# A two-layer block with routed experts: the first expert weight gather moved ahead of the row scatters, and the scattered rows normalised one chunk at a time

## The chip, the cores and the metric

The kernel runs on one core of a Trainium2 chip. The metric is the device time of one execution in microseconds (us). Three runs of the kernel before took 2112.46, 2118.58 and 2127.67 us, so the median is 2118.58 us.

The engines go by the short names of the profile: PE is the matrix engine, DVE the vector engine, ACT the scalar engine, POOL the general-purpose engine that here also issues all indirect (gathering and scattering) DMAs, and SP the engine that issues the plain ones.

## What is computed

The input is x, 8 sequences of 512 tokens with 256 features, in float32. There are two layers. Each normalises its input and adds an attention and a feed-forward part of the normalised rows to it. Layer 0, which the change touches, is cut to this:

```python
xn = layernorm(x)
x = x + attention(xn) + experts(xn)

# experts(xn), a row at a time
aff = xn @ centroids.T              # 8 experts
e = argmax(aff); alpha = sigmoid(aff[e])
h = layernorm(xn, ln_g[e], ln_b[e]) # a row that is normed a second time
y = xn + relu(h @ w1[e].T + b1[e]) @ w2[e].T + b2[e]
out = alpha * y + (1 - alpha) * xn
```

The second layer is two rounds of causal attention with a convolution between them, and a low-rank feed-forward part.

## The kernel before, in words

Tokens are held as 8 batches (`acc[b]`) of 4 chunks of 128 rows, 32 chunks in all. Layer 0 runs a fixed order of steps (`run`). Attention has 32 jobs (a batch and a group of four heads each) of 8 steps; job j's exponentials begin at step 12 + 8j, and its last product ends at step 20 + 8j. In each step the program issues score matmuls (L345 for the maxima, L394 for the exponentials), then `fill` puts other work into the step, then the products with the values (L434) follow. The work that `fill` takes comes from a list with due times (projections, transposed maxima) and from a generator, `stream`. The generator holds, in order: norms and affinities of the 8 batches (`FIRST`, 8 steps), `routing`, the experts, and the start of the second layer (`SECOND`). Where the generator yields `At(t)` nothing more is taken from it before step t; where it yields a number, that is a cost against an allowance of 2.08 a step. All engines work through their own instructions in the order of the program; waits between them are put in by the framework, one for each thing that an instruction needs.

**The rows that are scattered.** `first_norm` (L589) makes the once-normed rows of a batch on ACT (L257), and the twice-normed rows `h0` of four chunks on POOL (L596), into one of eight buffers that stay until the scatter. This happens in the first 53 us.

**Routing.** `routing` (L665) works out on DVE where each row goes (`pos_i`, L728) and which rows of the weight table each expert block needs (`wrow_i`, L738). Then, one chunk a step and 32 times, POOL issues an indirect DMA that scatters the 128 rows of the chunk to `hs_d` in DRAM (L741), and then a scaling of the chunk in place (`first_sum`, L608). Every scatter writes `hs_d`, and so the framework makes each wait for the one before it to land. At the same place in POOL's order stand the sums of finished attention jobs (L899).

**The experts.** When the 32 scatters have been issued, the pool `pre`, which holds `h0` among other things, is closed, and the pool `moe` takes its memory; a tile of `moe` waits for the tiles of `pre` that lay in its place. `Block(moe, 0)` (L753) issues on POOL the gather of the first block's weights (L756, 128 rows of 17,456 bytes) and on SP the load of its 256 rows of `hs_d` (L763). After `At(todo.t + 5)`, five steps later, `features` transposes these rows on PE (L772) and scales them on DVE with columns of the gathered weights (L777). `hidden` (L794, L805, L807) and `output` (L815, L824) follow. There are 23 blocks of 256 rows. The weights of block n + 1 are gathered while block n is worked on, in two buffers of `moe`. The sums of the blocks go to DRAM (L826), and `SECOND` gathers them back (L512), ends layer 0 and begins layer 1.

Of the kernel before, what the change touches and what calls it, by code (L numbers as in the profile page):

```python
# [9 lines left out]
F32 = mybir.dt.float32  # L10
# [3 lines left out]
ALU = mybir.AluOpType  # L14
# [5 lines left out]
P = 128  # L20
NB = 8
S = 512
D = 256
NC = S // P
# [26 lines left out]
ROW = O_B2 + D  # L51
# [101 lines left out]
def block_kernel(ctx: ExitStack, tc: tile.TileContext, x, a0_wqk, a0_bqk, a0_wv, a0_bv, cent, experts,  # L153
                 a1_wqk, a1_bqk, a1_wv, a1_bv, conv_w, conv_b, out_w, out_b, u1, v1, f_b1, u2, v2, f_b2, out):
    nc = tc.nc
# [11 lines left out]
    acc = []  # L167
# [13 lines left out]
    for i in range(2):  # L181
        half = mask_t[:, i * P : (i + 1) * P]
        nc.gpsimd.affine_select(
            out=half, in_=half, pattern=[[1, P]], compare_op=ALU.is_ge, fill=NEG, base=0, channel_multiplier=-1
# [18 lines left out]
    def bank(kind="mm"):  # L203
        rings[kind].append(rings[kind].pop(0))
        return rings[kind][-1]
# [12 lines left out]
    def banks_experts():  # L218
        share_banks(mx=banks[:2], sc=banks[4:6], av=banks[6:7], mm=banks[2:4] + banks[7:])
# [320 lines left out]
    wrow_i = const.tile([P, NBLK], I32, name="wrow_i")  # L540
# [24 lines left out]
    with ExitStack() as l0:  # L565
# [12 lines left out]
        nc.scalar.dma_start(out=cent_sb[:, :, :NE], in_=cent)  # L578

        later = ExitStack()  # L580
        pre = later.enter_context(tc.tile_pool(name="pre", bufs=1))
        aff = pre.tile([P, NT, NE], F32, name="aff")
        zeros = pre.tile([P, 2 * D], F32, name="zeros")
        nc.gpsimd.memset(zeros, 0.0)
        hs_z = hs_d.rearrange("(n p r) d -> n p (r d)", p=P, r=2)
        h0 = []
        firsts0 = {}

        def first_norm(norms, i):  # L589
            b = norms.bs[i]  # L590
            xn = work.tile([P, NC, D], F32, tag="o", name=f"xn{b}")
            norms.norm(i, xn)
            h = pre.tile([P, NC, D], F32, tag="h0", name=f"h0_{b}", bufs=NB)
            for c in range(NC):
                n = i * NC + c
                nc.gpsimd.tensor_scalar(  # L596
                    h[:, c, :], acc[b][:, c, :], norms.rs[:, 1, n : n + 1], norms.nm2[:, n : n + 1],
                    ALU.mult, ALU.add,
                )
                firsts0[b, c] = norms, n  # L600
            h0.append(h)
            return xn

        def first_sum(b, c):

            norms, n = firsts0[b, c]
            a = acc[b][:, c, :]
            nc.gpsimd.tensor_scalar(a, a, norms.rs1[:, n : n + 1], norms.nm_t[:, n : n + 1], ALU.mult, ALU.add)  # L608
# [27 lines left out]
        def pt(shape, name, tag=None, bufs=1):  # L636
            return pre.tile(shape, F32, name=name, tag=tag or name, bufs=bufs)
# [27 lines left out]
        def routing():  # L665

            mx = pt([P, NT], "mx")
            nc.vector.tensor_reduce(mx, aff, AX.X, ALU.max)
            nc.scalar.activation(alpha, mx, AF.Exp, scale=-1.0)
            nc.vector.tensor_scalar(alpha, alpha, 1.0, None, ALU.add)  # L670
            nc.vector.reciprocal(alpha, alpha)
            eq = pt(sh, "eq", "place")
            nc.vector.tensor_tensor(eq, aff, mx.unsqueeze(2).to_broadcast(sh), ALU.is_equal)
            cand = pt(sh, "cand", "rank")
            nc.vector.scalar_tensor_tensor(
                cand.rearrange(flat), eq.rearrange(flat), -float(NE), iota_e.rearrange(flat), ALU.mult, ALU.add
            )
            idx = pt([P, NT], "idx")
            nc.vector.tensor_reduce(idx, cand, AX.X, ALU.min)
            nc.vector.tensor_scalar(idx, idx, float(NE), None, ALU.add)  # L680
            oh = pt(sh, "oh")
            nc.vector.tensor_tensor(oh, iota_e, idx.unsqueeze(2).to_broadcast(sh), ALU.is_equal)
            yield At(todo.t + 1)


            ps = bank()
            psr, pst = ps[:, : NT * NE], ps[:, NT * NE :]
            nc.tensor.matmul(psr, lhsT=upper, rhs=oh.rearrange(flat), start=True, stop=True)
            nc.tensor.matmul(pst, lhsT=all_one, rhs=oh.rearrange(flat), start=True, stop=True)
            tot = pt(sh, "tot_sb")  # L690
            nc.vector.tensor_copy(tot.rearrange(flat), pst)
            cum = tot
            step = 1
            while step < NT:
                nxt = pt(sh, f"cum{step}", "cum", 2)
                nc.vector.tensor_tensor(nxt[:, step:, :], cum[:, step:, :], cum[:, : NT - step, :], ALU.add)
                nc.vector.tensor_copy(nxt[:, :step, :], cum[:, :step, :])
                cum = nxt
                step *= 2
            rank = pt(sh, "rank_sb", "rank")  # L700
            nc.vector.tensor_tensor(rank.rearrange(flat), cum.rearrange(flat), psr, ALU.add)
            yield At(todo.t + 2)

            gt = pt([P, NE, NB * S // TB], "gt")
            nc.vector.tensor_tensor(
                gt, cum[:, NT - 1, :].unsqueeze(2).to_broadcast([P, NE, NB * S // TB]), thr, ALU.is_gt
            )
            nblk = pt([P, NE], "nblk")
            nc.vector.tensor_reduce(nblk, gt, AX.X, ALU.add)
            ends = nblk  # L710
            step = 1
            while step < NE:
                nxt = pt([P, NE], f"ends{step}")
                nc.vector.tensor_tensor(nxt[:, step:], ends[:, step:], ends[:, : NE - step], ALU.add)
                nc.vector.tensor_copy(nxt[:, :step], ends[:, :step])
                ends = nxt
                step *= 2
            start = pt([P, NE], "start")
            nc.vector.tensor_tensor(start, ends, nblk, ALU.subtract)
            nc.vector.tensor_scalar(start, start, float(TB), None, ALU.mult)  # L720

            place = pt(sh, "place")
            nc.vector.tensor_tensor(place, rank, tot, ALU.subtract)
            nc.vector.tensor_tensor(place, place, start.unsqueeze(1).to_broadcast(sh), ALU.add)
            nc.vector.tensor_tensor(place, place, oh, ALU.mult)
            pos = pt([P, NT], "pos")
            nc.vector.tensor_reduce(pos, place, AX.X, ALU.add)
            nc.vector.tensor_copy(pos_i, pos)  # L728
            yield At(todo.t + 1)


            ge = pt([P, NBLK, NE], "ge")
            nc.vector.tensor_tensor(ge, iota_b, ends.unsqueeze(1).to_broadcast([P, NBLK, NE]), ALU.is_ge)
            wrow = pt([P, NBLK], "wrow")
            nc.vector.tensor_reduce(wrow, ge, AX.X, ALU.add)
            nc.vector.tensor_scalar(wrow, wrow, float(NE - 1), float(P), ALU.min, ALU.mult)
            nc.vector.tensor_scalar(wrow, wrow, iota_p, None, ALU.add)
            nc.vector.tensor_copy(wrow_i, wrow)  # L738

            for t in range(NT):  # L740
                nc.gpsimd.indirect_dma_start(  # L741
                    out=hs_d[:, :],
                    out_offset=IndirectOffsetOnAxis(ap=pos_i[:, t : t + 1], axis=0),
                    in_=h0[t // NC][:, t % NC, :],
                    in_offset=None,
                )
                first_sum(t // NC, t % NC)
                yield At(todo.t + 1)

        class Block:  # L750


            def __init__(self, moe, n):  # L753
                self.moe, self.n = moe, n
                self.w = moe.tile([P, ROW], F32, tag="w", name=f"w{n}")
                nc.gpsimd.indirect_dma_start(  # L756
                    out=self.w[:, :],
                    out_offset=None,
                    in_=experts,
                    in_offset=IndirectOffsetOnAxis(ap=wrow_i[:, n : n + 1], axis=0),  # L760
                )
                self.hs = moe.tile([P, TB // P, D], F32, tag="hs", name=f"hs{n}", bufs=1)
                nc.sync.dma_start(  # L763
                    out=self.hs, in_=hs_d[n * TB : (n + 1) * TB, :].rearrange("(j p) d -> p j d", p=P)
                )
# [64 lines left out]
        def stream():  # L830
# [7 lines left out]
            def norm(b):  # L838
                xns[b] = first_norm(*of[b])
# [17 lines left out]
            moe = later.enter_context(tc.tile_pool(name="moe", bufs=2, reuse_waits="tile"))  # L857
# [3 lines left out]
            nc.sync.dma_start(out=fb2_sb, in_=f_b2)  # L861
            nc.gpsimd.tensor_tensor(ob_sb, ob_sb, fb2_sb, ALU.add)
            nxt = Block(moe, 0)
            yield At(todo.t + 5)
            banks_experts()
            nxt.features()
            yield 0.5
# [18 lines left out]
        todo = Work()  # L886
# [48 lines left out]
        norms = [Norms(pre, bs, nm, True) for bs, nm in (((0,), "a"), ((1, 2, 3), "b"), ((4, 5, 6, 7), "e"))]  # L935
# [25 lines left out]
    with tc.tile_pool(name="ffn", bufs=1, side="right", reuse_waits="tile") as ffn:  # L961
# [53 lines left out]
        for n, (b, c2) in enumerate(pairs):  # L1015
# [6 lines left out]
            _, _, hT = ahead.pop(0)  # L1022
# [11 lines left out]
    for i in range(2):  # L1034
        t = l1.tile([P, 2, S + 2], F32, tag=f"ctxT{i}", name=f"ctxT{i}", bufs=1)
# [7 lines left out]
        out=cmask[:, S - P :], in_=cmask[:, S - P :], pattern=[[-1, P]], compare_op=ALU.is_ge, fill=NEG, base=0,  # L1043
# [224 lines left out]
```

## Time and profile before

The profiled execution took 2120.86 us. Its span, from its first instruction to its last, is 2118.7 us. The mean granted PE clock is 0.974 of full speed.

| engine | busy us | share of the span | instructions |
|---|---|---|---|
| PE, matmuls | 2010.6 | 95% | 13672 |
| DVE | 1228.6 | 58% | 3565 |
| ACT | 867.8 | 41% | 1690 |
| POOL | 175.6 | 8% | 222 |

| operation on or from POOL | count | mean us of one |
|---|---|---|
| L596, twice-normed rows of a chunk | 32 | 0.56 |
| L741, issue of a scatter | 32 | 1.04, landing 2.5 after its start (median) |
| L608, scaling of a chunk | 32 | 0.55 to 0.57 |
| L756, issue of a weight gather | 23 | 0.96, landing 9.5 after its start (median) |
| L899, sum of an attention job | 32 | 0.73 |

How to read it: an instruction is named by its line in the kernel, its engine and `out<-in`. An idle time is put down to what ended it. The chain of waits goes back from the last instruction: at each step to what released it. "issue" in it is time in which an engine waited for nothing that the profile shows. A DMA's issue is an instruction; its landing is later. DMA engines are shared by all queues.

### The profile page before, as it was taken

The numbers are of one execution on the slowest core, as the hardware profiler recorded it, in microseconds if no ns is written. First come the engines' busy times: TensorE is split into PE (matmuls) and PEld (weight loads), VectorE is DVE, ScalarE is ACT, GpSimd is POOL, SyncE is SP. The second block draws the span as 40 slices with busy tenths as digits, with TensorE's granted clock in tenths as the row PEclk, the third lists the DMA queues.
The fourth block names the chain that finished last, engine by engine and source line by source line (L and its number), as shares of the span: only waits on it lengthen the run. The fifth ranks groups of instructions, "written<-read, shape, count | busy, mean of one in ns | idle before, by whom it ended". The sixth has DMA issues, their size and how long they took to land.

```text
span 2118.7 us, 35530 instructions
## 1 busy us (share of the span) xinstructions
PE 2010.6 (95%) x13672; PEld 1016.4 (48%) x13672; DVE 1228.6 (58%) x3565; ACT 867.8 (41%) x1690; POOL 175.6 (8%) x222
## 2 busy tenths in 40 slices
PE   5797999999999999998898999999999999999998
PEld 3333555555555555552233445455555545554554
DVE  5564455555555555557424676666766666666763
ACT  4342333333333333335551444444444444444434
POOL 4153000000000000004211000000000000000000
PEclk8698999999999999999999899999999999999999
DMA  6014212212121221202100000000000000000000
GB/s 211 13 45 143 104 54 105 101 58 105 53 105 53 105 105 53 105 11 78 40 1 1 2 2 2 2 2 12 2 12 2 12 2 12 2 11 2 2 12 21
DMA packets 37192, 93.53 MB, mean 44 GB/s; under 512 B 5920, under 2 KB 28064, under 8 KB 34080
## 3 DMA queue, kind: packets, MB, share of 16 engines
q0 software_dynamic: 6384, 59.78, 7.7%
q1 hardware_dynamic: 29792, 30.56, 4.5%
q8 instruction: 107, 1.75, 0.3%
q10 hardware_dynamic: 848, 0.93, 0.1%
q14 instruction: 61, 0.50, 0.1%
HBM read 70.03 MB, written 20.45 MB: 43 GB/s over the span
## 4 chain that ended last, share of the span: by engine, by line
PE 83%; DVE 6%; issue 5%; DMA 4%; ACT 2%; POOL 1%; ACTq 0%; POOLq 0%; DVEq 0%; SPq 0%
PE bank L345 27%; PE bank L434 12%; PE bank L794 8%; PE bank L815 8%; PE bank L293 5%; PE bank L1072 4%; PE bank L412 4%; DMA hs_d<-h,pos_i 4%; PE bank L394 3%; PE bank L303 2%; PE bank L1090 2%; PE bank L1124 1%; DVE m L362 1%; PE bank L977 1%; PE bank L990 1%
## 5 line engine op out<-in xcount | busy, mean ns | idle before, releaser
L421 ACT ACTIVATE e<-bank 128x512 f32<-128x512 f32 (+1 forms) x1280 | 638.9, 552 | 921.4 <-PE bank L394 462.8
L345 PE MATMUL bank<-k,q 32*128 32x512 f32 (+3 forms) x3072 | 765.1, 538 | 24.6 <-DVE m L362 20.3
L394 PE MATMUL bank<-q,k 32*128 32x512 f32 (+3 forms) x3072 | 682.6, 535 | 2.4 <-DVE m L362 1.6
L365 DVE CUSTOM_DVE_ANT_0 jk<-bank,cmask 128x512 bf16<-128x512 f32 (+3 forms) x1024 | 502.8, 491 | 241.7 <-PE bank L345 162.4
L345 PEld LDWEIGHTS bank<-k,q 32*128 32x128 f32 x3072 | 301.4, 187 | 388.4 <-issue 165.2
L362 DVE TENSOR_REDUCE m<-bank 128x1 f32<-128x512 f32 x512 | 328.8, 685 | 152.5 <-PE bank L394 122.7
L434 PE MATMUL bank<-e,v 128*32 128x512 f32 (+3 forms) x3072 | 317.8, 501 | 0.7 <-ACT e L421 0.7
L394 PEld LDWEIGHTS bank<-q,k 32*128 32x128 f32 x3072 | 266.0, 186 | 12.2 <-issue 6.1
L794 PE MATMUL bank<-hsT,w 128*128 128x256 f32 x736 | 181.2, 392 | 6.4 <-DVE hsT L777 6.4
L794 PEld LDWEIGHTS bank<-hsT,w 128*128 128x128 f32 x736 | 135.1, 192 | 74.5 <-issue 58.9
L815 PE MATMUL bank<-w,hT 128*128 128x256 f32 x736 | 170.7, 385 | 0.0
L815 PEld LDWEIGHTS bank<-w,hT 128*128 128x128 f32 x736 | 137.5, 192 | 36.6 <-issue 18.7
L434 PEld LDWEIGHTS bank<-e,v 128*32 128x32 f32 x3072 | 67.7, 108 | 139.7 <-issue 133.0
L412 PE MATMUL bank<-mask_t,ident_bf 128*128 128x128 bf16 (+1 forms) x768 | 123.4, 244 | 0.0
L412 PEld LDWEIGHTS <-ident_bf 128*128 128x128 bf16 x768 | 43.9, 97 | 155.7 <-issue 140.6
L807 DVE TENSOR_SCALAR hT<-bank,w 128x256 f32<-128x256 f32 x92 | 44.5, 484 | 113.7 <-ACT hT L805 113.7
L1072 PE MATMUL bank<-ctxT,cw_sb 128*128 128x256 f32 x384 | 90.0, 383 | 2.1 <-DVE q L283 1.8
L365 DVE DVE_READ_ACCUMULATOR2_ANT m<- 128x1 f32 x1024 | 85.0, 83 | 0.0
L805 ACT ACTIVATE hT<-bank,w 128x256 f32<-128x256 f32 x92 | 43.7, 475 | 92.9 <-PE bank L794 92.9
L824 DVE TENSOR_TENSOR f<-bank,w 128x256 f32<-128x256 f32 x46 | 19.5, 425 | 105.4 <-PE bank L815 105.4
L285 ACT ACTIVATE k<-bank,bqk,rows 128x512 f32<-128x512 f32 x64 | 46.3, 774 | 81.7 <-PE bank L293 72.4
L1072 PEld LDWEIGHTS bank<-ctxT,cw_sb 128*128 128x128 f32 x384 | 70.1, 189 | 13.2 <-DVE q L283 3.2
(186 smaller groups left out, 1383.5 us busy)
## 6 DMA issues: line engine op xcount, KB each, us to landing
q<-mT SPq DMA_DIRECT2D x384, 2.0 KB
hs_d<-zeros SPq DMA_DIRECT2D x23, 256.0 KB
hs<-hs_d SPq DMA_DIRECT2D x23, 256.0 KB
fs_d<-f SPq DMA_DIRECT2D x23, 256.0 KB
acc<-in_x SPq DMA_DIRECT2D x8, 512.0 KB
out<-acc SPq DMA_DIRECT2D x8, 512.0 KB
cw_sb<-in_conv_w SPq DMA_DIRECT2D x1, 768.0 KB
wqk<-in_a_wqk ACTq DMA_DIRECT2D x1, 512.0 KB
```

What stands on the lines that cost most here:

```text
L285: nc.scalar.activation(dst, ps, AF.Identity, bias=bias[:, half : half + 1], scale=rows[:, half : half + 1])
L293: nc.tensor.matmul(ps, lhsT=w[:, k, col : col + P], rhs=src[:, k, :], start=(k == 0), stop=(k == 1))
L345: lambda h=h, qc=qc, at=at, nk=nk: nc.tensor.matmul(heads[h % 2][:, at : at + nk], lhsT=self.q[h * PH : (h + 1) * PH, qc * P : (qc + 1) * ...
L362: nc.vector.tensor_reduce(self.m[:, qc, h, :], src, AX.X, ALU.max, negate=True)
L365: nc.vector.tensor_tensor_reduce(out=junk[:, :nk], in0=src, in1=cmask[:, S - nk :], scale=1.0, scalar=-3e38, op0=ALU.add, op1=ALU.max, acc ...
L394: lambda h=h, kc=kc, at=at, lo=lo: nc.tensor.matmul(heads[h % 2][:, at : at + S - lo], lhsT=self.k[h * PH : (h + 1) * PH, kc * P : (kc + 1 ...
L412: nc.tensor.matmul(heads[h][:, : len(blocks) * P], lhsT=ident_bf, rhs=mask_t[:, : len(blocks) * P], start=False, stop=True,)
L421: nc.scalar.activation(e[:, h, :], heads[h][:, :n], AF.Exp, scale=self.scale)
L434: nc.tensor.matmul(self.av[h * PH : (h + 1) * PH, lo:], lhsT=self.v[:, kc, 4 * self.g + h, :], rhs=es[h // 2][:, h % 2, :], start=first, s ...
L794: nc.tensor.matmul(ps[:, i * TB : (i + 1) * TB], lhsT=w[:, O_W1 + k * FF + fc * P : O_W1 + k * FF + (fc + 1) * P], rhs=self.hsT[:, k, :], ...
L815: nc.tensor.matmul(ps[:, 0:D], lhsT=self.hT[:, fc, j * P : (j + 1) * P], rhs=w[:, O_W2 + fc * D : O_W2 + (fc + 1) * D], start=(fc == 0), s ...
L1072: nc.tensor.matmul(ps[:, :w], lhsT=cw_sb[:, k, tap, c * P : (c + 1) * P], rhs=ctxT[b % 2][:, k, tap + lo : tap + lo + w], start=(k == 0 an ...
```

## The change

The first expert block's weights get a pool of their own, `wp`, which is opened before `pre`. Their gather is issued right after `wrow_i` is made, ahead of the 32 scatters in POOL's order. The blocks' weights then alternate between one buffer in `wp` (even blocks) and one in `moe` (odd blocks). The 32 instructions at L596 leave `first_norm`; instead `norm_twice` makes the same rows chunk by chunk right before each scatter, into one of four buffers of one chunk. `features` of block 0 is allowed three steps after `Block(moe, 0)` where it was five.

```diff
+        wp = l0.enter_context(tc.tile_pool(name="wp", bufs=1))
...
-            h = pre.tile([P, NC, D], F32, tag="h0", name=f"h0_{b}", bufs=NB)
             for c in range(NC):
-                n = i * NC + c
-                nc.gpsimd.tensor_scalar(
-                    h[:, c, :], acc[b][:, c, :], norms.rs[:, 1, n : n + 1], norms.nm2[:, n : n + 1],
-                    ALU.mult, ALU.add,
-                )
-                firsts0[b, c] = norms, n
-            h0.append(h)
+                firsts0[b, c] = norms, i * NC + c
             return xn
+
+        def norm_twice(b, c):
+            norms, n = firsts0[b, c]
+            h = pre.tile([P, D], F32, tag="h0", name=f"h0_{b}_{c}", bufs=4)
+            nc.gpsimd.tensor_scalar(
+                h, acc[b][:, c, :], norms.rs[:, 1, n : n + 1], norms.nm2[:, n : n + 1], ALU.mult, ALU.add
+            )
+            return h
...
+            first_w.append(weights(wp, 0))
             for t in range(NT):
+                h = norm_twice(t // NC, t % NC)
                 nc.gpsimd.indirect_dma_start(
                     out=hs_d[:, :],
                     out_offset=IndirectOffsetOnAxis(ap=pos_i[:, t : t + 1], axis=0),
-                    in_=h0[t // NC][:, t % NC, :],
+                    in_=h,
                     in_offset=None,
                 )
                 first_sum(t // NC, t % NC)
                 yield At(todo.t + 1)
 
+        first_w = []
+
+        def weights(pool, n):
+            w = pool.tile([P, ROW], F32, tag="w", name=f"w{n}", bufs=1)
+            nc.gpsimd.indirect_dma_start(
+                out=w[:, :],
+                out_offset=None,
+                in_=experts,
+                in_offset=IndirectOffsetOnAxis(ap=wrow_i[:, n : n + 1], axis=0),
+            )
+            return w
...
-                self.w = moe.tile([P, ROW], F32, tag="w", name=f"w{n}")
-                nc.gpsimd.indirect_dma_start(
-                    out=self.w[:, :],
-                    out_offset=None,
-                    in_=experts,
-                    in_offset=IndirectOffsetOnAxis(ap=wrow_i[:, n : n + 1], axis=0),
-                )
+                self.w = first_w.pop() if n == 0 else weights((moe, wp)[n % 2 == 0], n)
...
             nxt = Block(moe, 0)
-            yield At(todo.t + 5)
+            yield At(todo.t + 3)
             banks_experts()
```

More of the change, by code (lines that the diff above doesn't have):

```diff
@@ L585, in block_kernel @@
         hs_z = hs_d.rearrange("(n p r) d -> n p (r d)", p=P, r=2)
-        h0 = []
         firsts0 = {}
```

## The prediction, made before the changed kernel ran

> **What bounds the kernel now.** I read the page first, then the chain of waits, the waits and POOL's timeline around 80 to 200 us, where the moved work lies.
>
> ```profile
> PE 2010.6 (95%) x13672; PEld 1016.4 (48%) x13672; DVE 1228.6 (58%) x3565; ACT 867.8 (41%) x1690; POOL 175.6 (8%) x222
> PE 83%; DVE 6%; issue 5%; DMA 4%; ACT 2%; POOL 1%; ACTq 0%; POOLq 0%; DVEq 0%; SPq 0%
> ```
>
> PE bounds the kernel as a whole. The 4% of DMA in the chain, some 80 us, are the 32 scatters, one after another. For most of that time PE has attention to do, so they cost only what PE stands idle at their end. The waits from 170 to 200 us:
>
> ```profile
> PE bank L794 <- DVE hsT L777: 6.4, 1, 6.4
> PE bank L772 <- DMA hs<-hs_d: 5.6, 1, 5.6
> ```
>
> PE stands twice: 5.62 us before the transposes of block 0, until its rows have come back from DRAM, and 6.44 us more before its first matmuls, as DVE's L777 needs the weights. Together 12.06 us. The chain of waits from 80 to 200 us (start, length, what):
>
> ```profile
> 109.39 2.65 DMA hs_d<-h,pos_i
> 112.08 0.71 issue
> 112.79 2.46 DMA hs_d<-h,pos_i
> ...
> 118.73 2.51 DMA hs_d<-h,pos_i
> 121.23 0.27 issue
> 121.50 2.46 DMA hs_d<-h,pos_i
> ...
> 181.59 2.45 DMA hs_d<-h,pos_i
> 184.19 2.60 DMA hs<-hs_d
> 186.92 1.10 PE bank L772 x4
> 188.02 5.78 issue
> 193.80 0.56 DVE hsT L777
> ```
>
> Each scatter starts when the one before has landed. Up to 112.79 the step between landing and start takes 0.71 us; from 118.73 on it takes 0.27. The rows of L741 show with what this goes:
>
> ```profile
> L741 POOLq EVENT_SEMAPHORE  x13: 17/17/41891, 45.6 to 115.3; - x13
> ```
>
> Thirteen separate wait instructions stand before scatters, the last at 115.3: the time of the 0.71 steps, and none after. POOL's timeline has the first sum of a job between the two kinds (117.60, L899), and the two gathers at the end:
>
> ```profile
> 117.60 0.72 POOL L899 TENSOR_TENSOR acc<-acc,og 128x256 f32<-128x256 f32 x1
> 118.73 1.03 POOL L741 DMA_INDIRECT hs_d<-h,pos_i  x1 [0.41 <-DMA hs_d<-h,pos_i]
> 119.81 0.55 POOL L608 TENSOR_SCALAR acc<-acc,rs1b,nmb 128x256 f32<-128x256 f32 x1
> 121.50 1.03 POOL L741 DMA_INDIRECT hs_d<-h,pos_i  x1 [1.14 <-DMA hs_d<-h,pos_i]
> ...
> 184.91 1.00 POOL L756 DMA_INDIRECT w<-in_experts,wrow_i  x1 [1.02 <-DMA hs_d<-h,pos_i]
> 185.93 0.74 POOL L899 TENSOR_TENSOR acc<-acc,og 128x256 f32<-128x256 f32 x1
> 186.83 0.97 POOL L756 DMA_INDIRECT w<-in_experts,wrow_i  x1 [0.16 <-issue]
> ```
>
> My reading, an inference: a scatter needs two things, the landing of its predecessor and the completion of POOL's own write of its rows. One fits into the instruction, the second takes a separate one, and the start comes 0.44 us later. Once POOL had waited for something younger than all rows (at the L899 of 117.60), the second was no longer asked for.
>
> **The change part by part.** Times are those of the profiled execution (2120.86 us; span 2118.7). It lies 2.3 us above the median of the three runs, 2118.58; I work out a difference and add it to the median.
>
> *What it removes.* The wait of 6.44 us: the weights are there long before. Left of it is DVE's first half of L777, 0.56 us and about 0.1 us to PE: 0.65. The 32 rows of L596 (17.4 us of POOL before 53 us) go too, worth nothing: POOL then waited 36.95 us before the first scatter, and who needs the rows is the scatter.
>
> *The gather in front.* `wrow_i` is done at 90.88 us (90.54 + 0.34). From the cast of `pos_i` (87.92 + 0.18 = 88.10) to the first scatter (88.97) POOL took 0.87 us, and a released scatter takes 0.27; so the gather starts between 91.15 and 91.75, I take 91.5. Its issue (1.0), the first rows (0.56) and the gap put scatter 0 at about 93.5; it was at 88.97. Then the queue. The gathers of 184.91 and 186.83 are followed by landings: L777 starts at 193.80, so the first needed no more than 8.9 us, and the shortest of all needed 8.7; the second took 12.5, to 199.3. That is 5.7 us behind the first though issued 1.9 behind it: it was served after it, not beside it. So scatter 0, in the same queue, lands after the gather (91.5 + 8.7 = 100.2) plus its own share (128 KB of the gather's 2.23 MB, 0.33 us): 100.5; scatter 1 starts at 101.25, where it was 92.38. Ends: no queueing, 93.5 + 2.5 + 0.7 = 96.7, or +4.3; or a full 2.5 behind the gather, +11. I take **+8.9**, by the pair of gathers, the nearest rows.
>
> The Trainium skill, page DMA: Bandwidth & Descriptors, section Rules for kernel authors, says to issue a DMA early and wait on its semaphore late, which would make this move free: the sum below would lose these 8.9 us. The same page, section Two DMAs through the same engine are not ordered, says descriptors of one queue start in order; the pair of gathers agrees, and no run here has a scatter behind a gather yet.
>
> *The rows chunk by chunk.* An instruction of 0.56 us now stands before each scatter. It lies in POOL's idle time of 1.1 us (1.57 with the long step), so it costs nothing itself; L899 and it together, 1.28, still fit into 1.57. Without that cover it would be 31 x 0.56 = 17.4 us. But the rows are now always POOL's youngest work, so I expect every scatter to keep its second wait: scatters 9 to 31, 23 steps, take 0.71 instead of 0.27: **+10.1**. Bounds: nothing if the separate wait is the early one (POOL's own, then over long before the landing), and 23 x (0.83 - 0.27) = 12.9 with the longest such step (from 184.04 + 0.04 to the gather at 184.91). I take 0.71, seen eight times in this very instruction.
>
> *The end of the scatters.* 8.9 + 10.1 = 19.0: the last lands at 203.0, the transposes of block 0 start at 186.92 + 19.0 = 205.9. Behind the scatters in POOL's order are the job sums L899; DVE needs them back two jobs later (16 steps of about 2 us), which covers 19 us. On SP the load of block 0's rows waits as before, with the transfer of a later job's row of maxima (L382, 184.66) behind it; PE stands before that job anyway. The second gather starts after the last landing and is first needed by block 1, whose first matmuls came 27 us after those of block 0 (222.0 and 194.45).
>
> *Three steps for five.* PE reached L772 at 181.30 (186.92 - 5.62). Two steps earlier it reaches it when the scores of step 47 end (L345 and L394 at 176.0 to 177.1): 177.1. The two steps are not lost, they follow later; but they no longer cover the wait.
>
> *Sum.* PE now stands from 177.1 to 205.9 = 28.8, and 0.65 before L794: 29.45, less 12.06: **+17.4 us**. From 260 to 945 us PE is 97 to 100% busy in the table of stretches, so nothing of it is caught up there. At the end of layer 0 the stream is two steps earlier against the attention; PE is idle 4.35 of 18 us there (1000 to 1018). Between nothing and -4.3 I take -1. In all +16.4, so 2118.58 + 16.4 = **2135 us**.
>
> **The rivals.**
>
> *A, the forecast: the scatters become the longer path by both terms,* 2135 us. For it: both delays stand in rows of this kernel, and the chain has no slack at its end, where PE already waits 5.62.
>
> *B, the gather delays the scatters, but the short step stays.* If POOL's own wait goes into the separate instruction, it is over before the landing. The scatters end 8.9 later: 17.4 - 10.1 - 1 = +6.3, 2125 us. Against it: in the first eight steps the old rows were done tens of us before, and the step was 0.71 all the same.
>
> *C, not slower: the scatters slip past.* With the DMA queue not holding the scatters up and the short step kept, only the 4.3 of the issue would remain, or nothing at all if part of the 0.71 steps of the first eight goes (8 x 0.44 = 3.5). Then PE stands 177.1 to 186.9 to 187.7, and 0.65: 10.5 to 11.3, so -1.6 to -0.8, with the tail of up to -4.3 in all 2113 to 2118. It decides from a delay of the last scatter under 1.5 us (12.06 - 0.65 - 9.8). Against it: 12.5 us for the second gather.
>
> *D, slower still: the new instruction is not hidden.* If it waited for the scatter before it, each step would take 0.56 more: +17.4 on top, about 2152 us. Against it: four buffers, so that its memory was free three scatters ago.
>
> **How the numbers follow.** A 0.62, B 0.2, C 0.06, D or another added wait 0.12. The three runs of before spread 15 us, so a median of a few is good to some 5. A's own range, with the gather's +4.3 to +11, the step's up to 12.9 and the tail, is 2127 to 2144. Eight in ten needs A, most of B and the near part of D: 2121 to 2146. One per cent, 21 us, is about what a measurement of this kernel can tell from no change; it lies at 2139.8. A passes it in about one case in five (0.12), D nearly always (0.11): slower 0.23; faster 0.01, from the far end of C; within 1% 0.76.
>
> **What would show it.** Of the profile after: the gather at 91 to 92 us and scatter 1 at 101 (right for the queue; at 97, wrong); "issue 0.71" between scatters up to the last (0.27: B); L741 with some 30 or more separate waits to about 200 us; the last scatter at about 200.6; PE's wait before L772 near 29 us and none before L794 but 0.7; about 4 us less work done by PE before that wait. Wrong would be: scatter steps of 3.7 us (D), or a scatter chain that ends before 187 us (C).

## The result, and the profile after

| | median us | runs | ratio to before, 95% interval |
|---|---|---|---|
| before | 2123.00 | 6, 2112.46 to 2130.49 | |
| after | 2151.09 | 6, 2143.07 to 2154.28 | 1.0121, 1.0093 to 1.0149 |

The change makes the kernel 1.2% slower. The forecast was 2135 us with a range of 2121 to 2146: the direction was right, the size was not. Of the miss, 4.4 us lie in the base: three further runs moved the median of before from 2118.58 to 2123.00. The forecast difference was +16.4 us; the ratio gives 0.0121 x 2123 = +25.7 (19.7 to 31.6).

The profiled execution took 2149.21 us, its span is 2147.4. The shares of the chain of waits, from the page after:

```profile
PE 82%; issue 7%; DVE 4%; DMA 4%; ACT 1%; POOL 1%; another core or an unknown queue 1%; POOLq 0%; DVEq 0%; ACTq 0%
```

DMA keeps its 4%, since the transfers of all scatters but the first two take as long as before; what lies between them counts as "issue". Most of the growth of "issue" from 5% to 7% costs nothing: it is POOL's idle time ahead of its first gather, 82.10 us from 8.55 on, where before it was 36.94 us from 52.03 on, as the rows of L596 no longer stand there. New is the 1% of "another core or an unknown queue", which the forecast had nothing for. The kernel runs on one core, so this is a wait of which the trace can't name the end. First the part that it did foresee: the chain of waits of the kernel after, at its beginning and its end (start, length, what):

```profile
92.07 0.56 POOL h L600
92.63 0.28 issue
92.91 7.17 DMA hs_d<-h,pos_i
...
100.12 0.71 issue
100.83 3.48 DMA hs_d<-h,pos_i
...
196.70 0.71 issue
197.41 2.46 DMA hs_d<-h,pos_i
...
200.61 2.45 DMA hs_d<-h,pos_i
...
203.08 2.66 DMA hs<-hs_d
205.74 0.14 issue
205.87 1.09 PE bank L781 x4
```

Scatter 0 starts at 92.91 and needs 7.17 us where a scatter alone needs 2.46: it was issued 2.0 us behind the gather of 90.90 and landed at 100.08. Then 0.71 stands before each scatter to the last but one, except three behind the sum of a job (124.76, 150.49 and 177.99 in the chain), where POOL's own work fills the step: the step from one scatter to the next is 3.2 to 3.4 us there, and 3.2 elsewhere. The line of the scatters in the kernel after shows with what:

```profile
L744 POOLq EVENT_SEMAPHORE  x35: 17/17/43, 90.7 to 199.9; - x35
```

Thirty-five separate waits to 199.9, where before had thirteen to 115.3. The other four stand before the first scatter, as five did in before. PE's waits from 165 to 215 us in the kernel after:

```profile
PE bank L781 <- DMA hs<-hs_d: 19.4, 1, 19.4
PE bank L345 <- DVE m L362: 7.0, 1, 7.0
```

The wait for the weights (6.44 us) is gone; the one for block 0's rows grew from 5.6 to 19.4. The 7.0 is earlier, at 174.4: DVE waits there for a sum on POOL.

```profile
DVE og L904 <- POOL acc L908: 6.6, 1, 6.6
```

That row is DVE's in the same stretch. POOL was behind with the sums of the attention jobs, because they stand behind the scatters in its order. By the order of the program this costs nothing on top: without it PE would have come to L781 sooner and stood there longer.

Where the rest went is seen by cutting the trace at fixed places of the work. Matmuls L434 come in the same order in all these kernels; this table, worked out from the traces, gives the us from the start of one to the start of another, by number. 0 to 256 holds the scatters and the first blocks, 256 to 896 the experts, 896 to 1152 the end of layer 0.

| kernel | 0 to 256 | 256 to 896 | 896 to 1152 |
|---|---|---|---|
| before; again | 223.3; 221.5 | 626.3; 626.3 | 300.5; 308.4 |
| after; again | 241.9; 241.6 | 623.9; 623.9 | 313.9; 311.1 |

From 1152 to 2944 all four take 827.7 to 827.8. So the head costs 18 to 20 us, of which 2.4 come back in the experts (PE is idle 2.1 us less there); and the end of layer 0, forecast at -1, costs 3 to 13, depending on which trace of before one takes. PE's idle time there varies less: 24.7 and 24.1 us of the end in the two traces of before, 33.6 and 32.0 in those of after, so 7 to 9.5 us more. PE stands twice there in the kernel after; its timeline:

```profile
977.79 1.22 PE L345 MATMUL bank<-k,q 32*128 32x512 f32 x1 [7.13 <-DVE m L362]
...
1005.88 1.22 PE L345 MATMUL bank<-k,q 32*128 32x512 f32 x1 [5.24 <-DVE m L362]
```

The chain of waits of the kernel after has the same two places:

```profile
970.01 7.01 another core or an unknown queue
...
1000.28 4.83 another core or an unknown queue
```

PE's granted clock falls with it. A stretch of the kernel after (us, PE, PEld, DVE, ACT, POOL busy, clock, DMA share, GB/s), then one at about the same place in the kernel before, 9 to 11 us behind number 896:

```profile
970.00:1010.00 40.00, 27.64 (x115) 7.87 (x111) 22.31 (x50) 11.45 (x21) 17.67 (x19) 0.72 0.21 60
```

```profile
952.00:990.00 38.00, 34.28 (x186) 10.63 (x183) 34.53 (x82) 17.25 (x32) 25.89 (x26) 0.97 0.29 84
```

In 40 us PE works 27.6 at a clock of 0.72; in before 34.3 of 38 at 0.97. So the stretches don't hold the same work: 40 of the products L434 start in the first and 56 in the second. In the kernel after the clock is 0.50 from 973.7 to 990.8 and from 1004.4 to 1018.1 and 1.00 between, so PE works at half speed for 12 to 13 us after the end of each stand: a group of eight products L434 takes 1.94 us at 981.83 and 988.57, and 1.07 before the stand.

### The profile page after: what moved, and what is told of

Its sections match the earlier page's. It is cut to its first block, busy times and chain, and to the rows that moved or that the text cites. A ratio compares the mean times of both kernels' runs of the same rounds, so it can differ in the third digit from the quotient of the medians.

```text
span 2147.4 us, 35536 instructions
## 1 busy us (share of the span) xinstructions
PE 2016.6 (94%) x13672; PEld 1017.3 (47%) x13672; DVE 1230.7 (57%) x3565; ACT 867.6 (40%) x1690; POOL 174.4 (8%) x222
## 4 chain that ended last, share of the span: by engine, by line
PE 82%; issue 7%; DVE 4%; DMA 4%; ACT 1%; POOL 1%; another core or an unknown queue 1%; POOLq 0%; DVEq 0%; ACTq 0%
PE bank L345 27%; PE bank L434 12%; PE bank L803 8%; PE bank L824 8%; PE bank L293 5%; PE bank L412 4%; PE bank L1081 4%; DMA hs_d<-h,pos_i 4%; PE bank L394 3%; PE bank L303 3%; PE bank L1099 2%; PE bank L1133 1%; PE bank L986 1%; PE bank L999 1%; PE bank L266 1%
## 5 line engine op out<-in xcount | busy, mean ns | idle before, releaser
L434 PE MATMUL bank<-e,v 128*32 128x512 f32 (+3 forms) x3072 | 320.1, 504 | 0.0
L434 PEld LDWEIGHTS bank<-e,v 128*32 128x32 f32 x3072 | 67.8, 109 | 142.5 <-issue 135.7
```

The costliest lines, as they stand in the source:

```text
L434: nc.tensor.matmul(self.av[h * PH : (h + 1) * PH, lo:], lhsT=self.v[:, kc, 4 * self.g + h, :], rhs=es[h // 2][:, h % 2, :], start=first, s ...
```

## The experiments

Three theories went into the runs. **T1**: the head costs what was forecast, and the stands at the end of layer 0 are a thing of their own. **T2**: they come from the three steps, with which the end of layer 0 meets the attention two steps earlier. **T3**: they fall into some executions of any kernel. Numbers such as 1.0115 are ratios to runs of the kernel before on the same chip (medians there 2120.1 to 2124.7). "Head" is the table's 0 to 256, "end" its 896 to 1152.

**r1_after_again**: no edit.

> The changed kernel once more, with nothing edited. T1 (the head costs some 16 us by the longer scatter chain; the two stands of PE at the end of layer 0, 7.1 us at 970.7 and 5.2 us at 1000.6, are something else): the head's rows come out the same to 0.2 us (scatter 1 at 101, last landing 203, PE's transposes of block 0 at 205.9). T2 (the stands come from the stream being two steps earlier against the attention): they are there again at 970 and 1000, and the time is 1.011 to 1.015 of before. T3 (the stands fall in some executions of any of these kernels): the profile may show none, and then its own time is near 2136 us.

Measured: 1.0115 (1.0078 to 1.0152). Stands of 6.30 us at 968.5 and 2.24 at 998.6; all dates of this trace lie 2 us earlier, since its first steps were shorter. The stand is no accident of one trace.

**e2_chunk_rows_only**: the kernel before with the change's `norm_twice` alone; the 32 instructions of L596 go.

```diff
+                h = norm_twice(t // NC, t % NC)
...
-                    in_=h0[t // NC][:, t % NC, :],
+                    in_=h,
```

> The kernel before, with the twice-normed rows made chunk by chunk and nothing else: the gather stays behind the scatters and the five steps stay. T1 (each scatter keeps a second wait because POOL's youngest work is its rows): 'issue 0.71' up to the last scatter, some 31 separate waits at the scatter's line, last landing at 184.04 + 10.1 = 194.2, PE stands 15.8 us before the transposes of block 0 and again some 6.4 us for the weights; in all +10 us (2133). Rival (the separate waits cost nothing, the whole delay of the change is the gather's): last landing at 184, 0 us. T2 expects no stands of PE near 970 and 1000 here, since the steps are those of before; T3 has them by chance.

Measured: 1.0053 (1.0023 to 1.0083), +11 us. Its waits of PE and the line of its scatters:

```profile
PE bank L773 <- DMA hs<-hs_d: 15.1, 1, 15.1
PE bank L795 <- DVE hsT L778: 6.9, 1, 6.9
```

```profile
L742 POOLq EVENT_SEMAPHORE  x36: 17/17/54697, 33.3 to 190.9; - x36
```

PE stands 22.0 where 22.2 was expected, and the head is 233.5, +11.2 on the mean of the two of before. The second wait is paid at every scatter. The end takes 303.1, with no stand of PE over 1.8 us.

**e3_three_steps_only**

```diff
-            yield At(todo.t + 5)
+            yield At(todo.t + 3)
```

> The kernel before, with block 0 allowed three steps after its loads where it was five, and nothing else. T1: PE reaches the transposes of block 0 at 177.1 where it was 181.3, and stands 9.8 us there and 6.4 us for the weights, so +4 us, given back in part at the end of layer 0 (0 to -4.3): 0 to +4. T2 (the earlier stream makes the stands of 7 and 5 us at the end of layer 0): they are there, and the time is +14 to +16 us. T3: the stands may or may not be there, as in every kernel.

Measured: 1.0053 (1.0030 to 1.0075), +11 us. The head is as T1 had it:

```profile
PE bank L772 <- DMA hs<-hs_d: 9.5, 1, 9.5
PE bank L794 <- DVE hsT L777: 6.5, 1, 6.5
```

But the end takes 308.8, and the stand is there, in the kernel before with one number changed. PE's timeline of this run:

```profile
958.15 1.02 PE L345 MATMUL bank<-k,q 32*128 32x512 f32 x2
965.59 1.22 PE L345 MATMUL bank<-k,q 32*128 32x512 f32 x1 [6.42 <-DVE m L362]
```

T2 holds, against T1's "0 to +4", though the +11 falls short of the +14 to +16 that it gave.

**e5_gather_behind**: the change, its first gather moved behind the scatters.

```diff
-            first_w.append(weights(wp, 0))
             for t in range(NT):
...
+                if t == NT - 1:
+                    first_w.append(weights(wp, 0))
```

> The changed kernel with its first weight gather issued right after the last scatter, still in its own home. T1: the scatter chain is that of the rows chunk by chunk alone, last landing at 194.2, nine us earlier than in the changed kernel; the gather is issued at about 192.8, and its weights come at about 201.5, when PE (which reaches the transposes at 177.1) has the rows at 197; PE stands 20 us for the rows and some 5 for the weights, in all +12 us, 4 us under the changed kernel. Rival (the gather in front costs the scatters nothing): the time of the changed kernel plus the wait for the weights. T2: two stands of PE at the end of layer 0, 12 us more.

Measured: 1.0126 (1.0089 to 1.0163); +12 was wrong, it is no better than the change. The chain of waits of this run shows why:

```profile
195.63 2.45 DMA hs_d<-h,pos_i
...
198.10 13.75 DMA hs<-hs_d
```

The scatters end at 198.1 (194.2 was expected), 5 us ahead of the change's, but the load of block 0's rows, issued on SP 0.7 us after the gather on POOL and 1.9 us ahead of block 1's, takes 13.75 us instead of 2.66. The Trainium skill, page DMA: Bandwidth & Descriptors, section Issuing engines are not separate DMA queues, says that transfers started by different engines run on the same 16 DMA engines; the 13.75 us agree. In the kernel before the rows' load goes out 0.7 us ahead of the first gather.

**e4_after_five_steps**: the change, its three steps undone.

```diff
-            yield At(todo.t + 3)
+            yield At(todo.t + 5)
```

> The changed kernel with the five steps put back; gather in front and rows chunk by chunk stay. The theory as it stands after the first four runs: three steps alone cost twice, some 4 us at the head (PE gets to block 0's transposes 4.2 us earlier and stands there) and 8 to 12 us at the end of layer 0, where the gathers of the block sums begin 5.6 us ahead of a job's row of maxima instead of 1.3, and the matmuls that need that row come 6 to 7 us late. So here: gathers of the block sums 1.3 us ahead of the row of maxima, no stand of 6 to 7 us at 960 to 1005, and 2151 - 4 - 10 = 2137 us. Rival (the stands are made by the longer head, not by the phase): they stay, and 2147 us.

Measured: 1.0100 (1.0063 to 1.0137), +21 us. No stand of PE over 1.8 us at the end, which takes 305.9: T2 again. The head is 235.1, 6.8 under the change's, yet the time fell by some 3 to 5 us, not by 14, and lies near the rival's 2147; 14 is at the edge of what the intervals of the two kernels allow. The trace is of an execution of 2139.44 us where the median is 2145.61, so its head and end flatter the kernel.

**e6_second_later**: the change, the end of layer 0 held back.

```diff
+            yield At(todo.t + 2)
             for pieces in SECOND:
```

> The changed kernel, and the end of layer 0 (the gathers of the block sums and all that follows them) held back by two steps; the head is untouched. Theory of the phase: the head's rows as in the changed kernel (transposes of block 0 at 205.9), the gathers begin 1.3 us ahead of a row of maxima as in the kernel before, the stand of 6 to 7 us is gone, and 2151 - 10 = 2141 us. Rival (the stand is made by the gathers wherever they lie, or by the head): it stays, and 2151 us or some 4 more for the two steps.

Measured: 1.0031 (1.0009 to 1.0054): some 18 us faster than the change with one line. The end takes 294.7, against 313.9 and 311.1. Not as expected: the gathers of the block sums still begin 5.6 us ahead of the row of maxima (POOL runs ahead to them), and a stand of 3.73 us is left. So the loss belongs to the order at the end of layer 0, but the phase of the gathers alone isn't it. Two reservations: the trace is of an execution of 2124.76 us where the median is 2131.23, and PE is still idle 29.4 us of its end; and three steps with the hold take less time than five without it (e4, 1.0063 to 1.0137), though e4's head is the shorter one. T2 alone doesn't give that.

**e7_rows_reversed**: the change, its rows made a batch ahead, last chunk first.

```diff
+            for c in reversed(range(NC)):
+                norm_twice(0, c)
             first_w.append(weights(wp, 0))
...
-                h = norm_twice(t // NC, t % NC)
+                if b + 1 < NB:
+                    norm_twice(b + 1, NC - 1 - c)
```

> The changed kernel, its rows still made during the scatters, but a batch ahead and in reverse order: the first scatter of a batch needs the youngest row, and the next three need older ones, for which no further wait is due. Theory (a scatter takes a second, separate wait only for a row younger than all that POOL has waited for, and it costs 0.44 us): 'issue 0.71' before every fourth scatter and 0.27 before the others, 23 x 0.44 = 10.1 us less, last landing near 193, transposes of block 0 at 195.8; the stands at the end of layer 0 stay as in the changed kernel, so 2151 - 10 = 2141 us. Rival (0.71 comes of the row's making lying between the scatters): 0.71 stays before each, and 2151 us. The gather in front, +8.9 on scatter 1, is seen alone here: scatter 1 at 100.8.

Measured: 1.0045 (1.0022 to 1.0069), some 15 us under the change. Its chain and its scatters:

```profile
92.38 7.90 DMA hs_d<-h,pos_i
100.28 0.27 issue
100.55 2.46 DMA hs_d<-h,pos_i
103.00 0.27 issue
103.27 2.43 DMA hs_d<-h,pos_i
105.70 0.27 issue
105.97 2.45 DMA hs_d<-h,pos_i
...
108.47 0.71 issue
```

```profile
L749 POOLq EVENT_SEMAPHORE  x12: 17/17/43, 90.7 to 181.1; - x12
```

One long step in four: the extra 0.44 us of issue is asked for by a row younger than all that POOL has waited for. The rows are still made between scatters, so it isn't their making. The gather's cost stands alone here: scatter 1 at 100.55. The head is 230.3, 11.6 less than the change's; the stand at the end (5.54 us) stays.

**e8_pieces**: e7 with five steps and the first gather cut in four, 32 partitions each.

```diff
+                if t in (20, 28, 29, 30):
+                    nc.gpsimd.indirect_dma_start(out=w0[32 * i : 32 * i + 32, :], ...)
```

> A version that keeps what the change was after without its two delays: rows a batch ahead in reverse order, the first weights gathered in four pieces of 32 partitions after the scatters 20, 28, 29 and 30, and the five steps. If a piece (a quarter of 8.7 us, some 2.2 us) fits between a scatter's rows and the next scatter, the scatters keep the steps of the kernel before but for some 0.5 us a piece: last landing at 184 to 187, transposes of block 0 at 187 to 190, no wait for the weights, so -5.8 us to -2 us of the kernel before: 2117 to 2122. Rival (each piece holds up the scatter after it by its whole length): +8.9 at the end of the chain, transposes at 195, and +3 us: 2127.

Measured: 1.0013 (0.9982 to 1.0044). The rival was right: scatters behind a piece took up to 4.5 us where 2.46 is usual, and block 0's transposes came 100.7 us after the first L434, where they come 101.7 after it with the whole gather in front (e7) and 93.4 in the kernel before. POOL's queue is as serial for pieces as for the whole. The trace has a stand of 6.53 us at 961.6 with five steps, the only one so long among those: T3 isn't empty.

**r2_before_again**: no edit, one run.

> The kernel before once more, nothing edited, for its trace of the end of layer 0. If the stands of 6 to 7 us are bound to three steps, none is here: PE is idle under 2 us at a time from 940 to 1000 as in the first trace. If they fall in any execution by chance, one of 3 to 7 us can show near 960 to 975.

Measured: 2125.46 us; no stand of PE over 1.2 us from 940 to 1000, yet the end takes 308.4, 7.9 more than in the first trace. The end of layer 0 varies by itself, and the first trace was at the good end. It isn't waiting that differs: PE is idle 24.7 and 24.1 us of the two ends, but the clock was granted at 0.50 for 41 us of the first and 51 us of the second, which by an estimate (ten more us at half the clock) is 5 of the 7.9 us. Over executions the time goes with the mean granted clock as well: on one chip the kernel before took 2107.00 us at 0.981 and 2139.46 us at 0.968. So the length of the end in a single trace says little, and PE's idle time in it more.

**e9_reversed_and_later**: e7 with e6's line.

> The changed kernel with two of the edits tried so far: rows a batch ahead in reverse order, and the end of layer 0 held back by two steps. If the two losses are separate things, their repairs add up: 2135 (rows reversed) less some 15 us (held back) is 2118 to 2120 us, a little under the kernel before. If holding back repaired something that the longer scatter chain caused, it does little here: 2131 to 2135 us.

Measured: 0.9986 (0.9963 to 1.0010). The two repairs add up; with both, the change is as fast as the kernel before. Its trace doesn't show it: it is of an execution of 2134.65 us where the median is 2122.47, and its end takes 308.8, of which PE is idle 27.8, with the clock at 0.50 for 65 us.

**e10_before_and_later**: e6's line in the kernel before.

> The kernel before with the end of layer 0 held back by two steps. If holding back only undoes what the three steps did (the end of layer 0 met the attention two steps early), here it makes the end two steps late: 0 to +6 us, 2123 to 2129. If it is a gain by itself (fewer gathers under way at a time), some -6 us or more: 2117 or less.

Measured: 0.9994 (0.9971 to 1.0017). Holding back is worth nothing where the three steps aren't. The trace has one wait of 3.4 us for a row of maxima.

**e11_last_first**: the kernel before, its scatters from the last chunk to the first.

```diff
+                s = NT - 1 - t
...
-                    in_=h0[t // NC][:, t % NC, :],
+                    in_=h0[s // NC][:, s % NC, :],
```

> The kernel before with its 32 scatters in reverse order, so that the first one needs the youngest row and no later one a wait for a row. Theory of the second wait: the eight early steps of 0.71 become 0.27, the chain ends 8 x 0.44 = 3.5 us earlier (last landing 180.5), PE stands 2.1 us for the rows and again 6.4 for the weights, and -3.5 us: 2120. Rival (the early steps are long for another reason, such as the early place): 0.71 stays in the first eight steps, 0 us.

Measured: 0.9982 (0.9956 to 1.0008), -4 us, which the interval doesn't tell from none. Its scatters have no wait after the first one:

```profile
L742 POOL DMA_INDIRECT hs_d<-h,pos_i x32: 1015/1025/1211, 86.9 to 174.3; - x32
L742 POOLq EVENT_SEMAPHORE  x5: 17/43/40717, 44.7 to 45.3; - x5
```

From the first scatter to the last it takes 87.4 us, 5.2 less than before (89.0 to 181.6); 3.5 of it were expected. PE stands only for the weights, 6.0 us, and the head is 217.4.

The last four ask what the stand is, and try what e10 and e11 point to.

**f1_gathers_later**: e6, and POOL reads a word that DVE writes ahead of the gathers.

```diff
...
+                    nc.vector.memset(token[:, 0:1], 0.0)
+                    nc.gpsimd.tensor_copy(token[:, 1:2], token[:, 0:1])
```

> The changed kernel with the end of layer 0 held back by two steps, as before, and a word that DVE writes at that place and POOL reads ahead of the gathers of the block sums, so that these cannot begin before it (until now they began as soon as the last block sum had landed, 5.6 us ahead of a row of maxima). If the row of maxima is late because it is sent into the gathers, they now begin after it, and the stand of PE at the first such row (3.7 us with the end held back, 7 without) is under 1.5 us; 2131 us or up to 4 less. If PE stands there anyway: 3.5 us or more once again.

Measured: 1.0056 (1.0033 to 1.0080). POOL's timeline of this run:

```profile
956.56 0.18 POOL L512 COPY token<-token 1x1 f32<-1x1 f32 x1 [8.15 <-DVE token L511]
957.38 1.00 POOL L516 DMA_INDIRECT fg<-fs_d,pos_i  x1 [0.64 <-issue]
```

The row of maxima goes out at 959.72, 2.3 us after the first gather and not 5.6, and the stand is gone; the end takes 298.2. But the time isn't under e6's (1.0031): what that last stand cost is less than the runs can tell.

**f6_rows_on_act**: the change, the rows of maxima (L382) sent from ACT's queue.

```diff
-                nc.sync.dma_start(out=self.q[...], in_=mT[4 * c : 4 * c + 4, :])
+                nc.scalar.dma_start(out=self.q[...], in_=mT[4 * c : 4 * c + 4, :])
```

> The changed kernel with the rows of maxima sent from ACT's queue where they were sent from SP's. If SP's queue is what holds the row up while the gathers run, the stands of 7 and 5 us are gone, 2140 us less what ACT loses by some 384 issues. If the gathers hold up what comes from any queue, or PE stands for another reason, they stay: 2151 us or more. It cannot tell the last two apart; f1_gathers_later can.

Measured: 1.0343 (1.0301 to 1.0384): layer 1 takes 881.4 us instead of 827.8, where ACT now issues the rows in the order of its own work; over the whole run ACT's exponentials wait 127.3 us for transfers of these rows. The end takes 302.5, with stands of 2.1 and 2.8 us where the change has 7.1 and 5.2. So the stands shrink when the row is sent from elsewhere; that the row itself is held up less isn't shown.

**f4_last_first_eight** and **f5_last_first_ten**: e11, block 0 allowed later.

```diff
-            yield At(todo.t + 5)
+            yield At(todo.t + 8)
```

and the same with 10. 

> The kernel before with its scatters in reverse order and block 0 allowed eight steps after its loads where it was five. In the run with reverse order alone PE stands only for the weights, 6.0 us; three more steps of attention are some 6 us of work for PE, so that wait goes, and the end of layer 0 has taken two steps' delay at no cost: 2118 - 5 = 2113 us. If the three steps are missing again at the end of layer 0: 2118 to 2122 us.

> The same with ten steps. Nothing is left to hide after eight, so the same 2113 us if the end of layer 0 has room for five steps, 2117 to 2123 if it has not.

Measured: 0.9990 (0.9971 to 1.0008) and **0.9921 (0.9897 to 0.9945)**, 2103.71 us against 2120.07: the one version that beats both kernels, by 16 us of the kernel before. With eight steps the stand for the weights only changes its name: the next row of maxima is sent on SP at 183.0, with the weights' gather under way, and attention waits for it until 192.2. With ten little is left. PE's waits from 165 to 215 us, with eight and with ten:

```profile
PE bank L394 <- DMA q<-mT: 4.8, 1, 4.8
```

```profile
PE bank L394 <- DMA q<-mT: 1.8, 1, 1.8
```

The heads are 211.3 and 200.7, the ends 308.4 and 306.9. The expectation of 2113 was wrong for both, in opposite directions. With eight steps most of what the head gains comes back as a loss in the experts: 631.7 against 626.3 in e11, so that head and experts together are only 0.8 us shorter. With ten the experts take 625.7, and nothing comes back. One thing that differs is POOL's order. With eight steps the gathers of blocks 0 and 1 go out at 179.64 and 181.55, both ahead of the row of maxima; with ten a second job's sum stands between them, and they go out at 178.76 and 193.69. What else lies in the 13.6 us between the two medians was not followed, nor was a run made that moves the second gather alone.

## Why the prediction was wrong

*The gather in front, +8.9.* Right: +8.45. Scatter 1 was forecast for 101.25 and started at 100.83 (92.38 before); e7 has the term alone. The prediction weighed the Trainium skill's advice to issue a DMA early (DMA: Bandwidth & Descriptors, Rules for kernel authors) against the pair of gathers; the 7.17 us of scatter 0 agree with the other section, Two DMAs through the same engine are not ordered, that descriptors within one queue of a DMA engine start in order.

*The rows chunk by chunk, +10.1.* Right: +10.6 from scatter 1 to the last landing, and +11.2 in e2's head. The step was read a little short: the chain shows 0.04 us of the wait itself beside the 0.71, so landing to start is 0.75 (112.04 to 112.79), 0.48 more than 0.27, and 23 x 0.48 = 11.0. The inference behind it is shown by e7 (one row in four, one long step in four) and e11 (no younger row, no long step). Rivals B and C are out with it. D, that the new instruction isn't hidden, is out too: the step is 3.2 to 3.4 us to the end, not 3.7.

*The end of the scatters.* Last landing forecast 203.0, measured 203.06; transposes 205.9, measured 205.87. That it fits this closely is luck in part, as the first term was 0.45 us too large and the second 0.5 too small.

*"which covers 19 us".* Wrong: the sums L899 were late, DVE waited 6.6 us for one, and PE stood 7.0 before its wait for the rows. It changed where PE stood, not how long the head was.

*Three steps, and PE's stand of 28.8 us.* Right in sum: 7.0 + 19.4 + 0.7 = 27.1 against 29.45 with the last half; head and experts together cost 15.9 to 18.0 us against +17.4.

*"Between nothing and -4.3 I take -1".* **This is the step that failed**, and in sign: the earlier stream was to fill idle time of PE at the end of layer 0, and PE's idle time there grew by 7 to 9.5 us. The lengths of the end: six traces with five steps (before twice, e2, e4, e11, and e10 with its hold) take 300.5 to 310.5, mean 305.8 (307.4 with e8's 317.5); five with three steps and without e6's hold of two steps (after twice, e3, e5, e7) 308.8 to 313.9, mean 311.7. That is +4 to +6 where -1 was taken. PE's idle time parts them better: 24.1 to 26.8 us with five steps (e8 32.7), 29.0 to 33.6 with three, a mean of 25.5 and of 31.4 without e8. e3 says the same by time: +11.3, of which head and experts account for 5.4. e4, where the steps are undone in the change itself, agrees by its trace, but not by its median. The working looked at PE's idle time as room to be filled; it did not ask what the earlier work would meet: a chain of a job's maxima (DVE, PE, SP and back to PE) that attention needs for its exponentials, and at which the stands lie. Nor did it price the clock behind a stand. Neither a rival nor the range held a loss there.

The sum is then 15.9 to 18.0 and 4 to 6: 20 to 24 us, against a measured 25.7 (19.7 to 31.6). What lies between is inside the interval and not explained further; the medians also differ in the mean granted clock, 0.962 to 0.969 in the six runs of after against 0.967 to 0.981 in those of before.

*What stays open.* Why PE stands 5.5 to 7 us in each of the five traces with three steps and no hold, and in one (e8) of the nine without the three steps. As far as f1 and f6 go, one run each, it needs the gathers under way for some 5 us and mostly goes when the row comes from another queue; but in the kernel before the second row of maxima goes out amid the gathers too and is waited for 0.8 us only. In the stands the traces lack many semaphore records, so which transfer ends them can't be read. Another order of the gathers with the row left where it is wasn't tried. And why the change with five steps (e4) isn't faster than with three and the hold (e6).

## What to carry to other kernels

A stage that lies beside the bottleneck is priced at its end: add up what is put into its chain (a transfer ahead in the same queue, a second wait at every link), and subtract only the stand that was there. Work that is moved earlier arrives earlier everywhere behind it; a place downstream where engines hand each other small results can lose by that, and "idle there" is no proof of room. And where one wait can cover several links, let the first link need the youngest data: reversing a loop (e11) took all second waits away, and with it moving the consumer back (f5) did what moving the producer forward (the change) did not.

## What the runs showed of the hardware

- From the landing of one scatter to the start of the next it took 0.75 us (0.71 of it after the separate wait) where the scatter waited for two things, and 0.27 where it waited for one, even if the second thing, a row, had been done for tens of us.
- A load of 256 KB on SP's queue took 13.75 us when a gather of 2.23 MB on POOL's queue had been issued 0.7 us earlier and a second followed 1.9 us later (e5), and 2.6 us when it went out ahead of them; a row of maxima, 8 KB in four pieces, was waited for until 9 us after its first issue in f4, behind two such gathers.
- The granted clock of PE was 0.72 over 40 us in which PE stood twice for 5 and 7 us, against 0.97 where it stood under 1.6 us at a time in the kernel before. It stayed at 0.50 for 12 to 13 us of work after the end of each stand, so the time after a stand is part of its price.
- The same kernel's end of layer 0 took 300.5 and 308.4 us in two executions, with no stand of PE over 1.8 us in either, and the clock at 0.50 for 41 and 51 us of it.
